# A perceiver layer on one core: tail loads merged and put before the last context slab, and two reorderings on TensorE

## The chip, the cores and the metric

The kernel runs on one core of a Trainium2 chip. A core has five engines that run side by side, each with its own list of instructions: TensorE (PE in the profile, with its weight loads as PEld), VectorE (DVE), ScalarE (ACT), GpSimd (POOL) and SyncE (SP). SP does no arithmetic here: it issues the loads, one after another, and a load that has to wait holds up all behind it. Sixteen DMA engines carry them out. The metric is the time of the whole program on the device in microseconds (us), lower is better.

## The reference: what is computed

Eight batches of 64 rows of 512 numbers (`x`) go through one layer, all in float32:

```
x = x + cross_attention(layernorm(x), context)      # one head of 512; context: 8 x 1601 rows of 512
x = x + resonance_attention(layernorm(x))           # 16 heads of 32, sigmoid in place of softmax
x = x + experts(layernorm(x))                       # 8 experts, each row goes to its best one
```

In the cross attention of a batch the scores are `(q Wq + bq)(ctx Wk + bk)^T / sqrt(512)`; a softmax runs over the 1601 context rows, and the result is the weighted sum of `ctx Wv + bv`. Only this part reads the context, 3.3 MB a batch, and it is where most of the change lies.

## The kernel before

The 512 rows of x are four tiles of 128 rows, so a tile holds a pair of batches (`p` = 0 to 3, `b2` = 0 or 1 in it). The projections with Wk and Wv are moved out of the context: the queries are multiplied by Wk (`keyed`), the scores are taken against the raw context, and the weighted sum of raw context rows is multiplied by Wv afterwards (`at_out`, matmuls named `p_po`).

**Context.** 1601 rows of a batch are 12 x 128 and 65 more. The first 1536 come in three slabs of 1 MB (`cx_p_g_b2`, groups g = 0, 1, 2), each 128 partitions by four rows. The 65 rest (group 3, the tail) are spread over four blocks of 32 partitions as 17, 16, 16 and 16 rows (`REST`) in a tile that POOL filled with zeros at the start (L205). Tails have two sets of tiles; pair p uses set p % 2.

**Loads.** `load_group` issues them on the SP queue. For pair 0 the order is weights and x, then the slabs of groups 0, 1, 2 (both batches each), then eight tail loads. For later pairs `load_pair` issues groups 0, 1, tails, 2. A slab's buffer comes from a pool of twelve, so a later load also waits until its buffer's last reader is done. Three tiny POOL copies named `held` (L931) stand between the first readings of two buffers and their reuse by pair 1.

**Transposes.** The scores need the context with its 512 columns on the partitions. DVE transposes 32 x 32 blocks (`turn_group`, L245 for slabs, L252 for tails) into tiles `T_p_q_b2`, q = 0 to 3 a quarter of the columns. A quarter's tile is complete when groups 0, 1, 2 and 3 are in it. For pair 0 the order of DVE's work at the beginning is written out by hand: groups 0 and 1 for all quarters, then groups 2 and 3 for quarters 0 and 1, and then for quarters 2 and 3 (`turn_first`).

**Scores.** `scores` (L411) multiplies quarter by quarter into four PSUM banks `sc`, the two batches in the two halves of the rows. For quarter 0 of pair 0 it does the first 256 columns of each bank early (groups 0 and 1) and the rest (`lo=256`: group 2 and the tail) later; between them PE computes `qb` (L379, `biased`).

**Softmax and sum.** `softmax` takes the maximum on DVE and the exponential on ACT into L. `chances` transposes a group of L on PE (L457, `pp`) and copies it to `pt` on ACT (L459). `attend` (L467, `ac`) multiplies it with the raw slabs. In the gap while ACT computes the exponentials, PE does other work: for p = 1 and 2 the projection of the pair before (`at_out`, L187), into whose middle the first `chances` is put.

**The other parts.** The steps of the second attention and of the experts (`unit_q`, `values`, `split`, `flip` and so on) run on tiles two pairs behind, between these. After pair 3 a list of `do(...)` lines gives PE's order: `split` transposes q and k (`t_q`, `t_k`), `flip` transposes rows that were gathered for the experts (`t_xe`), ACT copies them to `xeT` (L1087), and `up_first` multiplies them (`gu`, L1097). The rows come by DMA from a buffer in HBM, into which POOL scattered them, behind the loads of the expert weights (`fetch`, L1083).

PE's order is the program's text order throughout. DVE's and ACT's are so in marked stretches and are planned by the framework elsewhere.

Of the kernel before, what the change touches and what calls it, by code (L numbers as in the profile page):

```python
# [10 lines left out]
F32 = mybir.dt.float32  # L11
# [6 lines left out]
P = 128  # L18
B, S, D = 8, 64, 512
# [17 lines left out]
def perceiver_kernel(ctx: ExitStack, tc: tile.TileContext, out: bass.AP, t: dict):  # L37
    nc = tc.nc
# [8 lines left out]
    one = pool(name="one", bufs=1)  # L47
# [3 lines left out]
    def slab(name):  # L51
        return slabs.tile([P, DC, D], F32, tag="slab", name=name)
# [4 lines left out]
    def row4(name):  # L57
        return rowp.tile([P, DC, P], F32, tag="row", name=name)
# [54 lines left out]
    bq, _ = load_c("xbq", [P, DC], nc.scalar)  # L113
# [68 lines left out]
    def projected(srcT, w, name, between=None):  # L182
# [14 lines left out]

    scale = 1.0 / math.sqrt(D)
    tails = [
        [one.tile([P, D], F32, tag=f"tail{k}{b2}", name=f"tail{k}{b2}") for b2 in range(2)]  # L200
        for k in range(2)
    ]
    for k in range(2):
        for b2 in range(2):
            nc.gpsimd.memset(tails[k][b2], 0.0)  # L205


    REST = (17, 16, 16, 16)
    def load_group(p, g):
        got = []  # L210
        for b2 in range(2):
            src = t["ctx"][2 * p + b2]
            if g < 3:
                c = slab(f"cx_{p}_{g}_{b2}")
                rows = src[: 12 * P, :].rearrange("(q c) d -> q c d", c=12)
                ins = nc.sync.dma_start(out=c, in_=rows[:, 4 * g : 4 * g + 4, :])
                if p == 1 and g == 0:
                    tc.keep_in_program_order(ins)
            else:
                c = tails[p % 2][b2]  # L220
                k0 = 12 * P
                for a, n in enumerate(REST):
                    ins = nc.sync.dma_start(
                        out=c[32 * a : 32 * a + n, :], in_=src[k0 : k0 + n, :]
                    )
                    if p < 2:
                        tc.keep_in_program_order(ins)
                    k0 += n
            got.append(c)
        return got  # L230

    cxs = {}
    for g in (0, 1, 2, 3):
        cxs[0, g] = load_group(0, g)


    NB = D // 32
    WIDTH = tuple(384 + n for n in REST)

# [3 lines left out]
    def turn_group(T, p, q, b2, g):  # L243
        if g < 3:
            nc.vector.transpose(  # L245
                T[:, :, 128 * g : 128 * g + 128].rearrange("p b (c k) -> p b c k", k=32),
                cxs[p, g][b2][:, :, 128 * q : 128 * q + 128].rearrange(
                    "p c (b d) -> p b c d", d=32
                ),
            )  # L250
        else:
            ins = nc.vector.transpose(  # L252
                T[:, :, 384:416],
                cxs[p, 3][b2][:, 128 * q : 128 * q + 128].rearrange("p (b d) -> p b d", d=32),
            )
            if p > 1:
                tc.keep_in_program_order(ins)
# [71 lines left out]
        T = slabs.tile([P, DC, D], F32, tag="slab", name=f"T_0_{q}_{b2}")  # L329
        first[q, b2] = T[:, :, :416]  # L330

    def turn_first(g, qs=range(4)):
        for b2 in range(2):
# [10 lines left out]
    for g in (0, 1):  # L344
        turn_first(g)
# [48 lines left out]
    def queries(p):  # L394

        return one.tile([P, NB, P], F32, tag="R", name=f"R_{p}")
# [8 lines left out]
    def scores(p, q, R, sc, Ts, js=range(4), lo=0, hi=D):  # L405
        for j in js:
            b = 4 * q + j
            for a in range(4):
                for b2 in range(2):
                    r = b2 * S  # L410
                    nc.tensor.matmul(  # L411
                        sc[a][r : r + S, lo : min(hi, WIDTH[a])],
                        lhsT=R[32 * a : 32 * a + 32, b, r : r + S],
                        rhs=Ts[b2][32 * a : 32 * a + 32, j, lo : min(hi, WIDTH[a])],
                        start=(b == 0 and lo == 0), stop=(b == NB - 1),
                    )

    def softmax(p, sc):
# [13 lines left out]
        for a in range(4):  # L432
# [4 lines left out]
            )  # L437
        for a, n in enumerate(REST):
            nc.scalar.activation(
# [13 lines left out]
    def chances(p, g, L):  # L453
        nch = 4 if g < 3 else 1
        tp = bank4(f"pp_{p}_{g}")
        for j in range(nch):
            nc.tensor.transpose(tp[:, j, :], L[:, 4 * g + j, :], ident)  # L457
        pt = row4(f"pt_{p}_{g}")
        nc.scalar.copy(pt[:, :nch, :], tp[:, :nch, :])  # L459
        return pt  # L460
# [433 lines left out]
    def at_out(i, between=None):  # L894
        project(i, tile_of[i]["acT"], between)
# [7 lines left out]
    def load_pair(p):  # L903

        for g in (0, 1, 3, 2):
            cxs[p, g] = load_group(p, g)
# [4 lines left out]
    def do(*steps):  # L911
        for f, i in steps:
            f(i)
# [29 lines left out]
            for q in qs:  # L943
                turn_group(second[q, b2], 1, q, b2, g)

    for qs in (range(2), range(2, 4)):
        for g in (2, 3):
            turn_first(g, qs)
    scores(0, 0, R, sc, [first[0, 0], first[0, 1]], lo=256)
    first[3, 1] = blocks(0, 3, 1)  # L950
    for q in range(1, 4):
# [7 lines left out]
    for p in range(NT):  # L959
# [32 lines left out]
        r = over_sum()  # L992
# [4 lines left out]
        def chance():  # L997
            pts.append(chances(p, len(pts), L))
# [6 lines left out]
        if p == 0:  # L1005
            chance()
            tables()
            keep_keyed(1, qk)
            R = queries(1)
        elif p + 1 < NT:  # L1010
            R = queries(p + 1)
            if p == 1:
                qk = keyed(NT - 1)
            at_out(p - 1, chance)
            if p == 1:
                keep_keyed(NT - 1, qk)
        else:
            at_out(p - 1, chance)
        if 0 < p < NT - 1:
# [126 lines left out]
    fetch(0)  # L1146
    load_experts_late(gu, dn)
    do((unit_q, 2), (at_turn, 3), (unit_k, 2), (at_out, 3), (norm, 3), (gates, 2))
    do((values, 2), (flip, 0), (split, 2), (up_first, 0), (turn, 3), (align, 2), (up_last, 0))
    do((unit_q, 3), (over, 0), (sums, 2))  # L1150
    unit_k(3, lambda: back(2))
    do((flip, 1), (output, 2))
# [134 lines left out]
```

## Time and profile before

| | us |
|---|---|
| median of three runs (lowest, highest) | 288.14 (286.54, 288.61) |
| the profiled execution | 286.62 |
| its span, first to last instruction | 284.7 |
| PE busy in the span | 270.7 |
| DVE, ACT, POOL busy | 159.1, 113.4, 70.5 |
| clock that PE was granted | 0.998 of full speed |

The span is shorter than the time by 1.9 us, which lie around the first and the last instruction. Busy time says that an engine had an instruction running, not that it ran at its peak. An idle gap is given with what ended it ("<-DVE T L252" is: until DVE's instruction of line 252 wrote tile T). Names stand as output<-inputs; "x64" counts instructions; each float32 matmul of the program appears as two. A row of several instructions has been merged, and its time is from the first start to the last end.

### The profile page before, as it was taken

How to read it: one execution, taken by the hardware profiler on the slowest of the kernel's cores; microseconds unless marked ns; L12 is line 12 of the kernel's file. 1: busy time of each engine (PE TensorE's matmuls, PEld its weight loads, DVE VectorE, ACT ScalarE, POOL GpSimd, SP SyncE). 2: the span in 40 equal slices, each digit the busy share in tenths (PEclk: the TensorE clock that was granted, in tenths of full speed). 3: DMA queues.
4: the chain of work that ended last, by engine and by line, in shares of the span. 5: the costliest groups of instructions: out<-in, count | busy, mean ns of one | idle time of the engine just before them, and what ended most of it. 6: DMA issues, size and time to landing. Idle time of an engine off the chain costs nothing. (4 is left out here: it accounts for less than half of the span.)

```text
span 284.7 us, 6695 instructions
## 1 busy us (share of the span) xinstructions
PE 270.7 (95%) x2724; PEld 136.0 (48%) x2724; DVE 159.1 (56%) x422; ACT 113.4 (40%) x244; POOL 70.5 (25%) x120
## 2 busy tenths in 40 slices
PE   6999699999999999999999999999999999999990
PEld 5975548335643345644434564434444555442320
DVE  3576729359432987846688765631562476384130
ACT  2574006980176522267744047534326424130210
POOL 3351560000971004060220400031140041404211
PEclk9999999999999999999999999999999999999999
DMA  6997686399799980000897036299980200614501
GB/s 210 423 416 308 196 290 236 92 423 395 265 316 397 383 321 9 6 0 0 315 361 284 2 146 211 92 294 367 359 309 2 76 0 2 211 48 149 151 0 45
DMA packets 20177, 57.72 MB, mean 203 GB/s; under 512 B 2418, under 2 KB 10658, under 8 KB 16432
## 3 DMA queue, kind: packets, MB, share of 16 engines
q1 hardware_dynamic: 17568, 50.37, 48.2%
q0 software_dynamic: 2432, 6.89, 6.9%
q8 instruction: 23, 0.38, 0.6%
q14 instruction: 10, 0.08, 0.1%
q10 hardware_dynamic: 144, 0.00, 0.0%
HBM read 50.94 MB, written 6.84 MB: 203 GB/s over the span
## 5 line engine op out<-in xcount | busy, mean ns | idle before, releaser
L245 DVE STREAM_TRANSPOSE T<-cx 128x512 f32<-128x512 f32 x96 | 61.5, 678 | 19.0 <-DMA cx<-in_ctx_dram 18.6
L411 PE MATMUL sc<-T,R 32*64 32x400 f32 (+4 forms) x1088 | 48.1, 480 | 2.4 <-DVE T L252 2.3
L467 PE MATMUL ac<-cx,pt 128*64 128x512 f32 x192 | 43.8, 598 | 0.1
L411 PEld LDWEIGHTS sc<-T,R 32*64 32x64 f32 x1088 | 24.1, 131 | 21.0 <-issue 14.6
L401 ACT COPY R<-qkT 32x512 f32<-32x512 f32 x40 | 24.6, 616 | 0.7
L467 PEld LDWEIGHTS ac<-cx,pt 128*64 128x64 f32 x192 | 12.7, 136 | 22.2 <-issue 21.4
L1097 PE MATMUL gu<-wgu,xeT 128*32 128x512 f32 x192 | 22.8, 597 | 0.0
L544 POOL TENSOR_TENSOR gm_k<-qn_k,c_gk 128x512 f32<-128x512 f32 x4 | 5.1, 1282 | 60.0 <-DVE qn_k L539 60.0
L401 POOL COPY R<-qkT 32x512 f32<-32x512 f32 x24 | 14.5, 605 | 17.4 <-PE sc L411 10.9
L422 DVE TENSOR_REDUCE mx<-sc 128x1 f32<-128x400 f32 (+1 forms) x16 | 8.1, 568 | 13.5 <-PE sc L411 13.5
L187 PE MATMUL p_po<-w_xWv,acT 128*128 128x512 f32 x32 | 14.9, 592 | 0.0
L359 PE MATMUL qk<-qpT,w_xWkT 128*128 128x128 f32 (+1 forms) x96 | 14.8, 311 | 0.0
L187 PE MATMUL p_q<-w_aWq,xhT 128*128 128x512 f32 x32 | 14.8, 606 | 0.0
L187 PE MATMUL p_k<-w_aWk,xhT 128*128 128x512 f32 x32 | 14.7, 595 | 0.0
L315 PE MATMUL qp<-xnT,w_xWq 128*128 128x128 f32 (+1 forms) x64 | 14.5, 383 | 0.1
L187 PE MATMUL p_o<-w_aWo,cT 128*128 128x512 f32 x32 | 14.5, 596 | 0.0
L187 PE MATMUL p_v<-w_aWv,xvT 128*128 128x512 f32 x32 | 14.4, 592 | 0.0
L507 POOL TENSOR_TENSOR x<-x,c_bo 128x512 f32<-128x512 f32 x4 | 5.1, 1273 | 36.3 <-DVE xh L506 36.3
L359 PEld LDWEIGHTS qk<-qpT,w_xWkT 128*128 128x128 f32 x96 | 13.4, 191 | 1.4 <-issue 0.6
L459 ACT COPY pt<-pp 128x512 f32<-128x512 f32 (+1 forms) x16 | 8.2, 510 | 10.4 <-PE pp L457 10.3
L315 PEld LDWEIGHTS qp<-xnT,w_xWq 128*128 128x128 f32 x64 | 9.7, 191 | 4.5 <-ACT xnT L304 0.4
L1132 PE MATMUL y<-wd,hT 128*32 128x512 f32 x96 | 11.5, 596 | 0.3 <-ACT hT L1124 0.3
(197 smaller groups left out, 371.3 us busy)
## 6 DMA issues: line engine op xcount, KB each, us to landing
cx<-in_ctx_dram SPq DMA_DIRECT2D x24, 1024.0 KB, 8.5
wgu<-in_wgT_dram SPq DMA_DIRECT2D x8, 512.0 KB, 9.9
wgu<-in_wuT_dram SPq DMA_DIRECT2D x8, 512.0 KB, 7.1
wd<-in_wdT_dram SPq DMA_DIRECT2D x8, 512.0 KB
rd<-blank POOLq DMA_DIRECT2D x6, 258.0 KB, 6.1
in<-rd SPq DMA_DIRECT2D x6, 258.0 KB, 4.2
xd<-blank POOLq DMA_DIRECT2D x6, 256.0 KB, 5.8
in<-xd SPq DMA_DIRECT2D x6, 256.0 KB, 7.1
```

The lines of the kernel that those rows point to most:

```text
L187: nc.tensor.matmul(ps, lhsT=srcT[:, dc, :], rhs=w[:, dc, :], start=(dc == 0), stop=(dc == DC - 1),)
L245: nc.vector.transpose(T[:, :, 128 * g : 128 * g + 128].rearrange("p b (c k) -> p b c k", k=32), cxs[p, g][b2][:, :, 128 * q : 128 * q + 12 ...
L315: nc.tensor.matmul(ps[ec][:, : n * P], lhsT=wq[:, dc, ec * P : (ec + 1) * P], rhs=xnT[:, dc, cols], start=(dc == 0), stop=(dc == DC - 1),)
L359: nc.tensor.matmul(ps[c * n // DC][:, c % (DC // n), :, :], lhsT=wkT[:, ec, c * P : (c + 1) * P], rhs=qpT[:, ec, cols], start=(ec == 0), s ...
L401: copy(R[32 * a : 32 * a + 32, j::4, :], qkT[32 * j : 32 * j + 32, :, :])
L411: nc.tensor.matmul(sc[a][r : r + S, lo : min(hi, WIDTH[a])], lhsT=R[32 * a : 32 * a + 32, b, r : r + S], rhs=Ts[b2][32 * a : 32 * a + 32, ...
L422: nc.vector.tensor_reduce(mx[:, a : a + 1], sc[a][:, : WIDTH[a]], AX.X, ALU.max)
L459: nc.scalar.copy(pt[:, :nch, :], tp[:, :nch, :])
L467: nc.tensor.matmul(ac[r : r + S, :], lhsT=pt[:, j, r : r + S], rhs=cx[b2][:, j, :] if g < 3 else cx[b2], start=(g == 0 and j == 0), stop=( ...
L507: nc.gpsimd.tensor_tensor(xs[i], xs[i], bo, ALU.add)
L1097: nc.tensor.matmul(ps[c, :], lhsT=xTs[k][:, dc, c], rhs=ffw[e][0][:, dc, :], start=(dc == 0), stop=(dc == DC - 1),)
L1132: nc.tensor.matmul(y[c, :], lhsT=hT[:, ic, c], rhs=ffw[e][1][:, ic, :], start=(ic == 0), stop=(ic == IC - 1),)
```

## The change

Three edits. The first merges the two batches' tail tiles of a set into one tile `[128, 2, 512]`, filled by four loads (17, 16, 16, 16 rows by two batches) in place of eight. For pair 0 those four are issued ahead of the slab of group 2 of the second batch, and DVE's order there becomes: group 2 of batch 0 for quarters 0 to 2, tails of both batches for quarters 0 and 1, group 2 of batch 1 for quarters 0 to 2, tails for quarter 2, then quarter 3. Later pairs keep their order of groups. The second edit: for p = 2 the first `chances` follows the whole projection instead of standing in its middle; p = 1 and 3 stay. The third: `split` of tile 2 stands ahead of `flip` of the first gathered rows. In the built program, the instructions on PE, DVE, ACT, POOL and SP are otherwise in the same order; ACT's copy of `t_q` comes ahead of that of `t_xe`.

```diff
     tails = [
-        [one.tile([P, D], F32, tag=f"tail{k}{b2}", name=f"tail{k}{b2}") for b2 in range(2)]
-        for k in range(2)
+        one.tile([P, 2, D], F32, tag=f"tail{k}", name=f"tail{k}") for k in range(2)
     ]
     for k in range(2):
-        for b2 in range(2):
-            nc.gpsimd.memset(tails[k][b2], 0.0)
+        nc.gpsimd.memset(tails[k], 0.0)
...
+    def load_tails(p):
+
+        c = tails[p % 2]
+        k0 = 12 * P
+        for a, n in enumerate(REST):
+            ins = nc.sync.dma_start(
+                out=c[32 * a : 32 * a + n, :, :],
+                in_=t["ctx"][2 * p : 2 * p + 2, k0 : k0 + n, :].rearrange("b r d -> r b d"),
+            )
+            if p < 2:
+                tc.keep_in_program_order(ins)
+            k0 += n
+        return [c[:, b2, :] for b2 in range(2)]
+
     def load_group(p, g):
...
+        return [load_chunks(p, g, b2) for b2 in range(2)] if g < 3 else load_tails(p)
 
     cxs = {}
-    for g in (0, 1, 2, 3):
+    for g in (0, 1):
         cxs[0, g] = load_group(0, g)
+    cxs[0, 2] = [load_chunks(0, 2, 0)]
+    cxs[0, 3] = load_group(0, 3)
+    cxs[0, 2].append(load_chunks(0, 2, 1))
...
-    def turn_first(g, qs=range(4)):
-        for b2 in range(2):
+    def turn_first(g, qs=range(4), batches=range(2)):
+        for b2 in batches:
...
-    for qs in (range(2), range(2, 4)):
-        for g in (2, 3):
-            turn_first(g, qs)
+    turn_first(2, range(3), (0,))
+    turn_first(3, range(2))
+    turn_first(2, range(3), (1,))
+    turn_first(3, (2,))
+    for g in (2, 3):
+        turn_first(g, (3,))
     scores(0, 0, R, sc, [first[0, 0], first[0, 1]], lo=256)
...
-            at_out(p - 1, chance)
             if p == 1:
+                at_out(p - 1, chance)
                 keep_keyed(NT - 1, qk)
+            else:
+                at_out(p - 1)
+                chance()
...
-    do((values, 2), (flip, 0), (split, 2), (up_first, 0), (turn, 3), (align, 2), (up_last, 0))
+    do((values, 2), (split, 2), (flip, 0), (up_first, 0), (turn, 3), (align, 2), (up_last, 0))
```

`load_chunks(p, g, b2)`, which is not shown, issues one slab as `load_group` did.

More of the change, by code (lines that the diff above doesn't have):

```diff
@@ L199, in perceiver_kernel, with load_chunks @@
     tails = [
-        [one.tile([P, D], F32, tag=f"tail{k}{b2}", name=f"tail{k}{b2}") for b2 in range(2)]
-        for k in range(2)
+        one.tile([P, 2, D], F32, tag=f"tail{k}", name=f"tail{k}") for k in range(2)
     ]
     for k in range(2):
-        for b2 in range(2):
-            nc.gpsimd.memset(tails[k][b2], 0.0)
+        nc.gpsimd.memset(tails[k], 0.0)
     REST = (17, 16, 16, 16)
-    def load_group(p, g):
-        got = []
-        for b2 in range(2):
[L212 to L230, printed above, removed]
+    def load_chunks(p, g, b2):
+        c = slab(f"cx_{p}_{g}_{b2}")
+        rows = t["ctx"][2 * p + b2][: 12 * P, :].rearrange("(q c) d -> q c d", c=12)
+        ins = nc.sync.dma_start(out=c, in_=rows[:, 4 * g : 4 * g + 4, :])
+        if p == 1 and g == 0:
+            tc.keep_in_program_order(ins)
+        return c
+    def load_tails(p):
[7 more added lines that the diff above has]
+            if p < 2:
+                tc.keep_in_program_order(ins)
+            k0 += n
+        return [c[:, b2, :] for b2 in range(2)]
+    def load_group(p, g):
+        return [load_chunks(p, g, b2) for b2 in range(2)] if g < 3 else load_tails(p)
     cxs = {}
-    for g in (0, 1, 2, 3):
+    for g in (0, 1):
         cxs[0, g] = load_group(0, g)
+    cxs[0, 2] = [load_chunks(0, 2, 0)]
+    cxs[0, 3] = load_group(0, 3)
+    cxs[0, 2].append(load_chunks(0, 2, 1))
     NB = D // 32
@@ L330, in perceiver_kernel @@
         first[q, b2] = T[:, :, :416]
-    def turn_first(g, qs=range(4)):
-        for b2 in range(2):
+    def turn_first(g, qs=range(4), batches=range(2)):
+        for b2 in batches:
             for q in qs:
```

## The prediction

> **What bounds the kernel now.** I read the page first, then the waits of TensorE (PE), then the timeline around each wait, then the stretches of two microseconds with the DMA rate.
>
> ```profile
> PE 270.7 (95%) x2724; PEld 136.0 (48%) x2724; DVE 159.1 (56%) x422; ACT 113.4 (40%) x244; POOL 70.5 (25%) x120
> ```
>
> PE is busy for 270.7 of 284.7 us, so the kernel can only be shortened by what PE waits for: 14.0 us, of which 1.86 lie before the first matmul and about 6.5 behind the last. The list of its waits (total us, times, longest) names the rest:
>
> ```profile
> PE sc L411 <- DVE T L252: 2.3, 2, 1.5
> PE pp L457 <- ACT L L433: 0.8, 1, 0.8
> PE t_xe L179 <- DMA in<-xd: 0.6, 1, 0.6
> ```
>
> Each edit lies at one of these three. Together they hold 3.65 us, 1.3% of the time; that is the ceiling, unless an edit also moves a wait.
>
> **Edit 1: the tails.** The timeline around the first wait (start, duration, what, idle before it):
>
> ```profile
> 25.56 1.30 DVE L245 STREAM_TRANSPOSE T<-cx 128x512 f32<-128x512 f32 x2 [0.59 <-DMA cx<-in_ctx_dram]
> ...
> 28.47 0.81 PEld L379 LDWEIGHTS qb<-qpT,c_xbk 128*32 128x32 f32 x32 [0.39 <-issue]
> ...
> 28.74 1.31 DVE L245 STREAM_TRANSPOSE T<-cx 128x512 f32<-128x512 f32 x2 [1.88 <-DMA cx<-in_ctx_dram]
> ...
> 30.30 0.46 PE L411 MATMUL sc<-T,R 32*64 32x145 f32 x2 [0.74 <-DVE T L252]
> ...
> 31.90 0.51 DVE L252 STREAM_TRANSPOSE T<-tail 128x128 f32<-128x128 f32 x2 [1.47 <-DMA tail<-in_ctx_dram]
> ...
> 32.27 3.27 PEld L411 LDWEIGHTS sc<-T,R 32*64 32x64 f32 x126 [1.78 <-DVE T L252]
> ```
>
> PE has done all it can at 29.56 (L379's matmuls end there). It waits until 32.27 for the second batch's tail, which VectorE (DVE) sees at 31.90. The stretches say what the DMAs did meanwhile (last two columns: share of the 16 DMA engines, GB/s):
>
> ```profile
> 24.00:26.00 2.00, 2.00 (x8) 1.21 (x7) 1.41 (x3) 0.58 (x1) 0.00 (x0) 1.00 0.99 413
> 26.00:28.00 2.00, 2.00 (x58) 1.27 (x65) 0.87 (x2) 0.58 (x1) 0.00 (x0) 1.00 0.41 112
> 28.00:30.00 2.00, 1.55 (x56) 0.90 (x40) 1.26 (x3) 0.27 (x1) 0.00 (x0) 1.00 0.16 50
> ```
>
> All 16 engines run at 413 GB/s (25.8 each) until 26; then one or two are left. The SP queue's waits say why: its tail loads wait for context slabs to land, 25.3 us in 11 waits. An instruction list of the built program shows that every load waits for the eighth load before it, so the last tail load leaves only when the last slab has landed (28.74) and lands 3.1 us later.
>
> The change halves the tail loads (8 to 4 a pair, same 2 KB rows) and puts them ahead of the last slab. By the same counting the four now leave behind landings at 10.6 to 14.6, and the slab `cx_0_2_1` behind that of `cx_0_0_1` (16.9), all long before the queue runs dry. So the issue wait goes. What is late next is the slab, on the one engine that carries the odd rows. In the semaphore records a 17-row load has one late mark and a 16-row load has sixteen: the 17 rows sit on one engine. The packet records agree: from 27.0 to 29.7 rows of 2 KB follow one another every 83 ns.
>
> A slab lands every 2.5 us (16 engines of 64 KB at 25.8 GB/s). From the first at 14.6, the fifth (`cx_0_2_0`) is through at 24.6 on an engine without other work. Then that engine has 34 rows of the 17-row load and 6 of the other three: 80 KB, 3.2 us. Then its 64 KB of `cx_0_2_1`, 2.5 us. It lands at 30.3. The tails themselves land by about 28, and DVE turns them before the slab, in its new order. One transpose (0.67) ends at 31.0, and PE starts there instead of 32.27: **-1.25**. Behind it each quarter finds its tiles: this part takes PE about 1.1 us and a full quarter 2.8, DVE turns one tile in 0.67, and the tile built last ends at some 36, needed at 37.7.
>
> Bounds: nothing is won if the slab lands at 31.6 or later; all is won, 2.6 us (32.27 less 29.6), if the odd rows cost that engine nothing. I take 1.25, since it comes from rates measured in this very stretch.
>
> [...]
>
> Beside other work: the two big zero fills (L205) replace four; the first stands ahead of the identity on GpSimd (POOL), 1.05 us instead of 0.53, and the 15 idle turns (3.46 us, from 1.86) then end at 5.85. The transposes behind them start at 5.88, waiting for DVE. Cost 0, at most 0.5 if that cover is gone. Everything up to the second wait is paced by PE: pair 1's last slabs leave at 53.94 when PE has used a buffer, and its first ones at 30.48 when the `held` copies are through, 14 us before use. In the saturated stretch before the third pair, DVE has its first tiles by 104.6 and PE asks at 106.91: a slack of 2.3 us.
>
> **Edit 2: chances behind the projection (p = 2).**
>
> ```profile
> 125.99 1.88 PE L187 MATMUL p_po<-w_xWv,acT 128*128 128x512 f32 x4
> ...
> 128.63 0.65 PE L457 MATMUL pp<-ident,L 128*128 128x128 f32 x4 [0.75 <-ACT L L433]
> 129.12 1.88 PE L187 MATMUL p_po<-w_xWv,acT 128*128 128x512 f32 x4
> ...
> 129.37 0.59 ACT L459 COPY pt<-pp 128x512 f32<-128x512 f32 x1
> ...
> 131.80 3.65 PE L467 MATMUL ac<-cx,pt 128*64 128x512 f32 x16
> ```
>
> Four rows of `p_po` take 1.72 us from start to start. With all eight first, `pp` starts at 125.99 + 3.44 = 129.43; the last exponential ended at 128.49, so nothing waits. Then `pp` 0.49, `t_x` 0.43, the second `pp` 0.53 (starts as now), and `ac` starts at 130.88 instead of 131.80: **-0.92**. Its other condition is the copy of `pt`, which ends 1.33 us after `pp` starts: 130.76, just in time. If ScalarE (ACT) is late by more than 0.12, the excess is lost; bounds 0 and -0.92, taken -0.92. The add to x behind `p_po` comes 1.3 us earlier.
>
> **Edit 3: t_q and t_k ahead of t_xe.**
>
> ```profile
> 209.70 0.63 PE L179 MATMUL t_xe<-ident,in 128*128 128x128 f32 x4 [0.64 <-DMA in<-xd]
> ...
> 210.42 0.59 ACT L1087 COPY xeT<-t_xe 128x512 f32<-128x512 f32 x1 [2.61 <-PE t_xe L179]
> ...
> 211.13 2.06 PE L1097 MATMUL gu<-wgu,xeT 128*32 128x512 f32 x16
> ```
>
> `gu` starts 1.43 us after `t_xe`, because ACT copies in between; today `t_q` and `t_k` (0.44 each) fill just that gap. After the change they fill the wait for the rows, and the gap is bare. PE is free at 208.9 (205.46 + 8 x 0.43). New: `t_q` 208.9, `t_k` 209.34, `t_xe` 209.8, `gu` 211.23: **+0.10**. Had the rows landed by 208.9, it would cost 0.9; if they land after 209.8, 0. The rows move with PE, since the stream of expert weights that they queue behind starts at 184.03 when PE releases a buffer.
>
> **Sum.** -1.25 - 0.92 + 0.10 = -2.07 us. The profiled execution took 286.62 us (span 284.7 and 1.9 around it): 284.6. It lies 1.5 below the median of the three other runs (288.14); against the mean of all four, 287.5, the forecast is **285.4 us**.
>
> **Rivals.**
> 1. The odd rows don't hold the slab up. For: only 50 GB/s move after 28, so room is there; against: the one late mark. -2.6 - 0.92 + 0.1 = -3.4: 284.1.
> 2. The change doesn't do what it says at the tails: that engine is hit by something else (ring 8 moved 16 KB in 1.2 us at 29.45) and the slab lands at 31.6. Only edits 2 and 3 are left, -0.8: 286.7.
> 3. The gain sinks at `t_xe`: if the weights' stream is bound by DMA and not by PE, the rows land no earlier, and `gu` starts where it did: 287.5. For: the stream runs at 294 to 367 GB/s in three slices of the page; against: its start at 184.03.
> 4. Slower: the 40 rows ahead of the slab take longer than 83 ns. In the crowd at 26.5 to 26.9 single ones took 150. At that rate the slab lands at 24.6 + 6.0 + 2.5 = 33.1, PE starts at 33.8, +1.5 - 0.8 = +0.7: 288.2. It decides from 133 ns a row, where the loss reaches the 0.8 of the others.
>
> **Chances and range.** Forecast 0.48; rival 1 0.20; 2 0.12; 3 0.10; 4 0.10. A measurement of this kernel tells about 1% (2.9 us) from no change; its four runs span 2.1 us. Faster by over 1%: rival 1 in most cases and the upper edge of the forecast, 0.24. Slower by over 1% needs rival 4 at more than twice its price: 0.07. Within: 0.69. The range 283.2 to 288.0 goes from rival 1 with the lower runs of the kernel to rival 3; it leaves out most of rival 4 and the far ends of the scatter.
>
> **What would show it.** Right: one PE wait of about 1.4 us in front of `sc`, released by the transpose of `cx`, not of `tail`; DMA share near full until 27; no wait at `pp`; `ac` 4.9 us behind the start of `p_po`; no wait at `t_xe` but one of some 0.8 at `gu` on ACT. Wrong: `sc` running on from L379 without a wait, a wait there past 32.3, or a longer wait at `t_xe`.

## The result

| | before | after |
|---|---|---|
| median of 20 runs each, us | 286.71 | 288.15 |
| lowest, highest | 284.76, 288.61 | 286.14, 290.21 |
| the profiled execution | 286.62 | 289.25 |
| its span | 284.7 | 287.1 |

The ratio is 1.0059 with a 95% interval of 1.0033 to 1.0085: the change makes the kernel about 0.6% slower. (The ratios, here and below, are those on record; they aren't the quotients of the medians beside them.) Forecast were 285.4 us and a range that ends at 288.0.

The page of the kernel after, its line of busy times and one of its lines of 40 slices:

```profile
PE 273.6 (95%) x2724; PEld 138.6 (48%) x2724; DVE 159.3 (55%) x422; ACT 113.3 (39%) x244; POOL 70.4 (25%) x118
...
PEclk9999779999999999999999999999999999999998
```

PE is busy for 273.6 us where it was for 270.7, with the same 2724 matmuls. The row PEclk says why: in two slices of 7.2 us, from 28.7 us on, it had 0.7 of its clock.

The list of PE's waits in the kernel after:

```profile
PE sc L415 <- DVE T L249: 2.4, 2, 2.2
...
PE sc L415 <- DVE T L256: 0.7, 1, 0.7
PE gu L1107 <- ACT xeT L1097: 0.7, 1, 0.7
```

The waits at `pp` and `t_xe` are gone. At `sc` there are 3.1 us of waiting where there were 2.3, and the long one is now for the transpose of a slab (L249), not of a tail (L256). The timeline around it (start, duration, what, idle before it):

```profile
27.10 1.90 DVE L249 STREAM_TRANSPOSE T<-cx 128x512 f32<-128x512 f32 x3 [2.02 <-DMA cx<-in_ctx_dram]
...
30.02 0.89 DVE L256 STREAM_TRANSPOSE T<-tail 128x128 f32<-128x128 f32 x4 [1.02 <-DMA tail<-in_ctx_dram]
...
30.39 0.46 PE L415 MATMUL sc<-T,R 32*64 32x145 f32 x2 [0.68 <-DVE T L256]
...
32.28 1.90 DVE L249 STREAM_TRANSPOSE T<-cx 128x512 f32<-128x512 f32 x3 [1.36 <-DMA cx<-in_ctx_dram]
...
33.05 6.82 PE L415 MATMUL sc<-T,R 32*64 32x145 f32 x126 [2.20 <-DVE T L249]
...
39.80 0.33 PE L395 MATMUL t_qb<-ident,qbT 128*128 128x128 f32 x1
```

Two things went wrong. The slab `cx_0_2_1` lands at 32.25 (semaphore record), so PE starts the second part of `sc` at 33.05 instead of 32.27: 0.78 later than before. And the 126 matmuls that follow take 6.82 us; before, the same 126 took 3.96:

```profile
32.27 3.96 PE L411 MATMUL sc<-T,R 32*64 32x145 f32 x126 [1.52 <-DVE T L252]
```

The stretches of two microseconds of the kernel after (PE, PEld, DVE, ACT, POOL busy, then PE's granted clock, share of the DMA engines, GB/s):

```profile
31.00:33.00 2.00, 0.00 (x0) 0.00 (x0) 0.72 (x2) 0.00 (x0) 2.00 (x5) 0.79 0.71 156
33.00:35.00 2.00, 1.96 (x63) 1.96 (x71) 2.00 (x5) 0.00 (x0) 1.54 (x3) 0.50 1.01 408
35.00:37.00 2.00, 2.00 (x36) 1.44 (x31) 1.99 (x6) 0.00 (x0) 0.00 (x0) 0.50 0.96 270
37.00:39.00 2.00, 2.00 (x32) 1.42 (x24) 0.45 (x1) 0.00 (x0) 0.31 (x1) 0.50 1.00 381
39.00:41.00 2.00, 2.00 (x48) 0.88 (x40) 0.16 (x1) 0.00 (x0) 2.00 (x2) 1.00 0.45 144
```

From 32.2 to 39.0 us PE had half its clock (the clock's own record). In the profile of before, the wait ends at 32.27 and every stretch there shows 1.00.

So the profiled execution sums up as +0.78 (slab), +2.86 (clock), -0.98 (edit 2) and -0.09 (edit 3): +2.57, against a last matmul that ends 2.61 later. The two GB/s columns show the slab's lateness beginning much earlier. Before, from 24 to 27 us:

```profile
24.00:25.00 1.00, 1.00 (x5) 0.60 (x4) 0.97 (x2) 0.58 (x1) 0.00 (x0) 1.00 1.00 418
25.00:26.00 1.00, 1.00 (x5) 0.60 (x4) 0.44 (x1) 0.00 (x0) 0.00 (x0) 1.00 0.99 408
26.00:27.00 1.00, 1.00 (x18) 0.42 (x25) 0.87 (x2) 0.33 (x1) 0.00 (x0) 1.00 0.70 185
```

and after:

```profile
24.00:25.00 1.00, 1.00 (x4) 0.57 (x3) 1.00 (x2) 0.58 (x1) 0.00 (x0) 1.00 1.16 211
25.00:26.00 1.00, 1.00 (x5) 0.59 (x4) 0.08 (x1) 0.00 (x0) 0.00 (x0) 1.00 0.88 248
26.00:27.00 1.00, 1.00 (x14) 0.42 (x20) 0.00 (x0) 0.17 (x1) 0.00 (x0) 1.00 1.03 330
```

The engines are as busy as before and move half as much. This is not one engine with a queue of odd rows, which was my picture: all of them are slow. Packets of 8 KB of the slabs, which take 309 to 321 ns at 21 to 23 us, took 540 to 850 ns when they began at 24 to 25 us, and the slab ahead of the tails, `cx_0_2_0`, lands at 27.08 instead of 25.54. A slab has sixteen marks in the semaphore records, and its landing is the last. Fifteen marks of `cx_0_2_0` come by 24.35 before and by 25.17 after; the last one lags behind the others in both kernels, by 1.2 us from 20.6 us on. That this comes from a packet of 16 KB of the instruction queue, which the DMA records show at 16.4 us before and 16.8 after, is read from the order of times. The experiments ask three things: what each edit does alone, why the stream slows down, and what the clock is worth.

### The profile page after: what moved, and what is told of

Its sections match the earlier page's. It is cut to its first block, busy times and chain, and to the rows that moved or that the text cites. A ratio compares the mean times of both kernels' runs of the same rounds, so it can differ in the third digit from the quotient of the medians.

```text
span 287.1 us, 6661 instructions
## 1 busy us (share of the span) xinstructions
PE 273.6 (95%) x2724; PEld 138.6 (48%) x2724; DVE 159.3 (55%) x422; ACT 113.3 (39%) x244; POOL 70.4 (25%) x118
## 5 line engine op out<-in xcount | busy, mean ns | idle before, releaser
L249 DVE STREAM_TRANSPOSE T<-cx 128x512 f32<-128x512 f32 x96 | 61.5, 679 | 20.2 <-DMA cx<-in_ctx_dram 19.8
L415 PE MATMUL sc<-T,R 32*64 32x400 f32 (+4 forms) x1088 | 51.0, 506 | 3.1 <-DVE T L249 2.4
L415 PEld LDWEIGHTS sc<-T,R 32*64 32x64 f32 x1088 | 25.9, 141 | 22.7 <-issue 15.9
L405 ACT COPY R<-qkT 32x512 f32<-32x512 f32 x40 | 24.6, 616 | 0.7
```

What stands on the lines that cost most here:

```text
L249: nc.vector.transpose(T[:, :, 128 * g : 128 * g + 128].rearrange("p b (c k) -> p b c k", k=32), cxs[p, g][b2][:, :, 128 * q : 128 * q + 12 ...
L405: copy(R[32 * a : 32 * a + 32, j::4, :], qkT[32 * j : 32 * j + 32, :, :])
L415: nc.tensor.matmul(sc[a][r : r + S, lo : min(hi, WIDTH[a])], lhsT=R[32 * a : 32 * a + 32, b, r : r + S], rhs=Ts[b2][32 * a : 32 * a + 32, ...
```

## Experiments: each edit alone

The first three runs each make one edit of the diff and leave the rest as before.

> Edit 1 alone; edits 2 and 3 are taken back. Theory A (the loss is all in the tails: the slab behind the odd rows lands later than the last tail did, 0.8 us, and the longer wait of TensorE is followed by a window of some 6.8 us at half clock, 2.9 us): 2.5 to 3.7 us slower than before in the executions that show the half clock, about 0.8 slower in those that don't; one such window visible between 33 and 40 us. Theory B (the loss comes from edits 2 or 3): within 1 us of before.

Measured: median 288.06 against 287.05 (35 runs of before), ratio 1.0057 (1.0025 to 1.0090). Edit 1 alone costs as much as all three edits together. Theory A holds in direction and place; its 2.5 to 3.7 us for the executions with half clock came out as some 1.1 against before's with it and 2.6 against before's without. Its waits at `sc` are 2.2 and 0.8 us, its slabs land at 27.16 and 32.18, and its profile has half a clock for 3.4 us from 33.8.

> Edit 2 alone. Theory A: 0.9 us faster than before, no wait of TensorE at the first pp of p = 2, clock as before. Theory B: as slow as or slower than before.

Measured: 284.87, ratio 0.9949 (0.9917 to 0.9981). The wait at `pp` is gone, and this edit alone is a gain of half a per cent, 0.5 to 2.4 us by the interval. Predicted were 0.9.

> Edit 3 alone. Theory A: within 0.3 us of before; the wait at t_xe (0.64) is gone and one of some 0.7 stands at gu behind the copy xeT. Theory B: slower by up to 2 us.

Measured: 286.77, ratio 0.9995 (0.9964 to 1.0026): no difference that can be told. The wait at `t_xe` is gone, and one of 0.7 us at `gu` stands in its place. The three ratios together make no change, where the whole change has 1.0059; with intervals of 0.3% each, that difference isn't clear of the noise.

## Experiments: the odd rows

The next run makes all three edits, but issues the odd row by itself, so that no load has 17 rows:

```diff
-        for a, n in enumerate(REST):
+        at = [(32 * a, k0 + 16 * a + (a > 0), 16) for a in range(4)] + [(16, k0 + 16, 1)]
+        for r0, k0, n in at:
```

> The changed kernel with all three edits, but the 17-row load of each tail split into 16 rows and 1 row, so that no DMA engine carries 34 rows; five loads a pair in place of four, same bytes. Theory A (the odd rows on one engine hold the last slab up, and the long wait brings the half clock): cx_0_2_1 lands by 29.5 instead of 32.3, TensorE waits under 1 us in front of the second part of quarter 0, no half-clock window, 2.5 to 3.5 us faster than before and 4 to 5 faster than the changed kernel's profiled execution. Rival C (the slab is late for another reason: the instruction fetch on one engine, or its later issue): it lands at 31 to 32 as in the changed kernel, and the half clock stays.

Measured: 284.61, ratio 0.9946 (0.9912 to 0.9979). `cx_0_2_1` lands at 30.51 instead of 32.25 and PE starts at 31.30, so the 17-row load on one engine costs 1.74 us. But the slab lands later than theory A's 29.5, the wait at `sc` is 1.4 us and not under 1, and the gain is 1.5 us by the ratio where 2.5 to 3.5 were expected. The rate is no better either (220 GB/s from 23 to 26 us) and `cx_0_2_0` still lands at 27.28. So there are two troubles: the odd rows, and something in all the tail loads.

Another run keeps edit 2 alone of the others, and puts the merged tails, odd row apart, behind both slabs, with DVE's order to match:

```diff
-    cxs[0, 2] = [load_chunks(0, 2, 0)]
+    cxs[0, 2] = load_group(0, 2)
     cxs[0, 3] = load_group(0, 3)
-    cxs[0, 2].append(load_chunks(0, 2, 1))
```

> A version from what the runs showed: edit 2, the merged tail tile with its odd row as a load of its own (five loads a pair), but for pair 0 behind both slabs of group 2 as in the kernel before, and VectorE turning the tiles of quarter 0 first; edit 3 left out. Theory A with E or F (tails in the stream cost the slabs 1.6 us, the odd rows 1.8, the waits for earlier loads the rest): cx_0_2_0 lands at 25.5 and cx_0_2_1 at 28.7 as before, the tails by 29.5, TensorE starts the second part of quarter 0 by 30.3, 2 us earlier than before; with edit 2 the sum is 2.5 to 3.5 us faster than before, 283.6 to 284.6. If the tails land no earlier than 31 us, only edit 2 is left: 285.9 to 286.2.

Measured: 285.18, ratio 0.9949 (0.9921 to 0.9978). `cx_0_2_0` lands at 25.28, `cx_0_2_1` at 29.46, the last tail at 30.25 (before: 31.78), the last two later than theory A had them, and PE waits once at `sc`:

```profile
30.91 4.90 PE L414 MATMUL sc<-T,R 32*64 32x145 f32 x128 [1.05 <-DVE T L255]
```

PE starts 1.36 us earlier than before, but takes 4.90 us for what it then did in 4.42 (0.46 and 3.96), with gaps in between, and `t_qb` is only 0.42 earlier. Neither this version nor the one with the odd row apart is measurably better than edit 2 alone; where the latter's gain goes is told at the end.

## Experiments: why the stream slows down

All runs of this section are the changed kernel with other loads of the tails; only the traffic is compared. Each was run and profiled once (284.0 to 286.7 us). How far one profile can be trusted is seen where the same loads were profiled more than once: before, edit 2 alone, edit 3 alone and the filled kernel before (e6_before_filled, below) have 408 to 418 GB/s from 23 to 26 us and land the slabs at 25.49 to 25.64 and 28.72 to 28.92; the change, edit 1 alone and the filled change (e5_filled) have 238 to 270 GB/s, 26.96 to 27.16 and 32.05 to 32.25. The first has one load of 64 rows of each batch, to every other partition:

```diff
-        for a, n in enumerate(REST):
-            ins = nc.sync.dma_start(
-                out=c[32 * a : 32 * a + n, :, :],
-                in_=t["ctx"][2 * p : 2 * p + 2, k0 : k0 + n, :].rearrange("b r d -> r b d"),
-            )
+        ins = nc.sync.dma_start(
+            out=c[0:P:2, :, :],
+            in_=t["ctx"][2 * p : 2 * p + 2, k0 : k0 + 64, :].rearrange("b r d -> r b d"),
+        )
```

> The changed kernel with the four tail loads of a pair replaced by one load of 64 of the 65 rows of both batches to every other of the 128 partitions; same row size, the odd row left out, and the rows stand at other places than the computation needs (the tail's part of the scores and sums is another one). Theory E (the tails slow the whole stream because each load writes to 16 neighbouring partitions only): 400 GB/s and more hold through 23 to 27 us, cx_0_2_0 lands by 25.6 and cx_0_2_1 by 29. Theory F (rows of 2 KB with their own order slow it, wherever they go): the rate falls to 150 to 250 GB/s around 24 us as in the changed kernel, and cx_0_2_0 lands at 27.

One load to every other partition leaves the stream as it was: 412 GB/s from 23 to 26 us, the slabs at 25.81 and 28.92, and no wait for a tile at `sc` above 0.2 us. My first reading was that rows to neighbouring partitions are slow (theory E). The next two have four loads of 16 rows, to every eighth partition, and as the change has them:

```diff
-        for a, n in enumerate(REST):
+        for a in range(4):
...
-                out=c[32 * a : 32 * a + n, :, :],
+                out=c[a:P:8, :, :],
```

> The changed kernel, its tail loads replaced by four loads of 32 rows each (16 rows of each batch) that go to partitions a, a + 8, a + 16, ..., so to every eighth partition; the odd row of each batch is left out and the rows stand at other places than the computation needs, so only the traffic is meant. Theory E (rows that go to neighbouring partitions slow the whole stream): 400 GB/s or more from 23 to 26 us as before the change, cx_0_2_0 lands by 25.8 and cx_0_2_1 by 29.0 us, no wait at sc above 1 us. Theory F (any four loads of 2 KB rows between the slabs do it, wherever the rows go): 150 to 350 GB/s from 24 to 26 us, cx_0_2_0 lands at 27 and cx_0_2_1 at 30 or later, a wait at sc of about 2 us.

```diff
-                out=c[32 * a : 32 * a + n, :, :],
+                out=c[32 * a : 32 * a + 16, :, :],
```

> The control: the same four loads of 32 rows, to 16 neighbouring partitions each, as the change has them; the odd row of each batch is left out. Theory E and theory F alike: 150 to 350 GB/s from 24 to 26 us, cx_0_2_0 lands at about 27.1 and cx_0_2_1 at about 30.3 us. If instead it lands by 29.0 with 400 GB/s kept, it is the odd rows in the 17-row load alone that slow the stream, and both theories fall.

Theory E fell: every eighth partition slows the stream too (262 GB/s, 27.09 and 30.50), though less than neighbours do (204 GB/s, 27.77 and 31.00, later than either theory had it).

F met its bounds for the stream and the slabs there; the wait at `sc` was 1.1 us, not 2. Then four loads to every fourth partition, and one load to 64 neighbours:

```diff
-                out=c[a:P:8, :, :],
+                out=c[a:64:4, :, :],
```

> As the run with every eighth partition, but the 16 rows of each of the four loads go to every fourth partition (a, a + 4, ..., a + 60); the odd row of each batch is left out and the rows stand at other places than the computation needs. With every eighth partition the rate fell to 223 GB/s at 24 to 25 us and the slab landed at 30.50, so neighbouring partitions alone are not the cause. Theory G (a load of 16 rows is slow where its rows fall on few of the memory's paths, and both 16 neighbours and every eighth do that while every fourth doesn't): 400 GB/s or more from 23 to 26 us, cx_0_2_0 lands by 25.8 and cx_0_2_1 by 29.0 us, no wait at sc above 1 us. Theory F (small loads of 16 rows of 2 KB slow the stream wherever their rows go): 150 to 350 GB/s from 24 to 26 us, cx_0_2_0 lands at about 27 and cx_0_2_1 at about 30.5 us.

```diff
-            out=c[0:P:2, :, :],
+            out=c[0:64, :, :],
```

> One load of 64 rows of each batch in place of four, to the 64 neighbouring partitions 0 to 63; the odd row of each batch is left out and the rows stand at other places than the computation needs. Theory E (neighbouring partitions): 150 to 350 GB/s from 24 to 26 us, cx_0_2_0 at about 27, cx_0_2_1 at 30 us or later. Theory F (small loads) and theory G (few paths) alike: 400 GB/s or more until 26 us, cx_0_2_0 lands by 25.8 and cx_0_2_1 by 29.0 us, as the one load to every other partition did (25.81 and 28.92).

Every fourth partition is slow as F has it, but less (332 GB/s, 26.38 and 29.98); G's bounds are missed, and its paths are a supposition that no run shows. The single load to 64 neighbours is slow too (272 GB/s, 26.59 and 30.21), against F and G both. So it can't be only that the loads are small, and not the neighbours alone either. Four loads to every seventh partition came next:

```diff
-                out=c[a:P:8, :, :],
+                out=c[a : a + 106 : 7, :, :],
```

> As the runs with every eighth and every fourth partition: four loads of 16 rows of each batch, here to every seventh partition (a, a + 7, ..., a + 105); the odd row of each batch is left out and the rows stand at other places than the computation needs. [...] Theory F (four small loads cost more than one, wherever the rows go): as with every eighth or fourth partition, cx_0_2_0 at 26.4 to 27.1 and cx_0_2_1 at 30.0 to 30.5 us.

Measured: 325 GB/s, 26.73 and 29.83, far from the one load to every other partition (412, 25.81 and 28.92); F missed its last bound by 0.2 us. The places of the one harmless load were then filled by four loads and by two:

```diff
-                out=c[a:P:8, :, :],
+                out=c[2 * a : P : 8, :, :],
```

> The same places as the one load to every other of the 128 partitions (which left the stream at 412 GB/s from 23 to 26 us and landed the slabs at 25.81 and 28.92), but filled by four loads of 16 rows of each batch, each to every eighth partition (0, 2, 4 and 6 onwards). The odd row of each batch is left out and the rows stand at other places than the computation needs. Theory H (what counts is that all the rows together fall evenly on all parts of the memory): 380 GB/s or more from 23 to 26 us, cx_0_2_0 by 26.1 and cx_0_2_1 by 29.4 us. Theory F (small loads between the slabs disturb the stream wherever they go): at most 340 GB/s, cx_0_2_0 at 26.4 to 27.2 and cx_0_2_1 at 29.7 to 30.6 us.

```diff
-        for a in range(4):
+        for a in range(2):
...
-                out=c[2 * a : P : 8, :, :],
-                in_=t["ctx"][2 * p : 2 * p + 2, k0 : k0 + 16, :].rearrange("b r d -> r b d"),
+                out=c[2 * a : P : 4, :, :],
+                in_=t["ctx"][2 * p : 2 * p + 2, k0 : k0 + 32, :].rearrange("b r d -> r b d"),
```

> The same places again, filled by two loads of 32 rows of each batch, each to every fourth of the 128 partitions (0 and 2 onwards). The odd row of each batch is left out and the rows stand at other places than the computation needs. Theory H: as the one load, 380 GB/s or more, 25.8 to 26.1 and 28.9 to 29.4 us. Theory F: between the one load and four, 340 to 390 GB/s, cx_0_2_0 at 26.0 to 26.6 and cx_0_2_1 at 29.3 to 29.9 us.

By four loads: 318 GB/s, 26.39 and 29.67. By two: 410 GB/s, 25.71 and 28.85. So evenness of the sum (H) isn't enough, and the step from two loads to four, which F expected to be gradual, is a jump. What was left: it counts where the rows of each load by itself go, or loads of 16 rows are bad anywhere (F). Four loads again, moved by 32 partitions against e11_step4:

```diff
-                out=c[a:64:4, :, :],
+                out=c[32 + a : 96 : 4, :, :],
```

> The four loads to every fourth partition again (there 0 to 63: 332 GB/s from 23 to 26 us, slabs at 26.38 and 29.98), shifted by 32 partitions (32 + a, 36 + a, ..., 92 + a) and nothing else. [...] The odd row of each batch is left out and the rows stand at other places than the computation needs. [...] Theory F (loads of 16 rows disturb the stream wherever they go): at most 345 GB/s, cx_0_2_0 at 26.3 or later and cx_0_2_1 at 29.6 us or later.

And two loads of 32 rows, as in e17_two, but to every other of the partitions 0 to 63:

```diff
-                out=c[2 * a : P : 4, :, :],
+                out=c[a:64:2, :, :],
```

> [...] The odd row of each batch is left out and the rows stand at other places than the computation needs. [...] Theory F: as the two loads before, 380 GB/s or more, cx_0_2_0 by 26.0 and cx_0_2_1 by 29.2 us.

These two decide it. The stretch from 23 to 26 us with four loads to the partitions 0 to 63, every fourth:

```profile
23.00:26.00 3.00, 3.00 (x11) 1.81 (x10) 2.18 (x4) 0.73 (x2) 0.00 (x0) 1.00 1.04 332
```

and with the same four loads moved by 32 partitions, to 32 to 95:

```profile
23.00:26.00 3.00, 3.00 (x11) 1.81 (x10) 2.38 (x5) 0.75 (x2) 0.00 (x0) 1.00 1.02 412
```

The last column goes from 332 to the full 412 GB/s, and the slabs land at 25.75 and 28.87. Nothing but a start of 32 was added. Two loads of 32 rows to half the partitions, every other from 0 to 63, which F took for harmless:

```profile
23.00:26.00 3.00, 3.00 (x11) 1.80 (x10) 2.23 (x4) 0.77 (x2) 0.00 (x0) 1.00 1.08 254
```

They land the slabs at 27.07 and 30.62. F missed all its bounds in both runs, so what counts here is where the rows of each load go. By the rate:

| partitions of a load | loads | GB/s, 23 to 26 us | `cx_0_2_0` | `cx_0_2_1` |
|---|---|---|---|---|
| before: no tails there | 0 | 414 | 25.54 | 28.72 |
| every other of 128 (e7_spread) | 1 | 412 | 25.81 | 28.92 |
| every fourth, 32 to 95 (e18_shift) | 4 | 412 | 25.75 | 28.87 |
| every fourth of 128 (e17_two) | 2 | 410 | 25.71 | 28.85 |
| every fourth, 0 to 63 (e11_step4) | 4 | 332 | 26.38 | 29.98 |
| every seventh (e13_step7) | 4 | 325 | 26.73 | 29.83 |
| every eighth, 0, 2, 4, 6 (e16_four) | 4 | 318 | 26.39 | 29.67 |
| 64 neighbours (e12_one64) | 1 | 272 | 26.59 | 30.21 |
| the change: 16 neighbours, odd rows on one engine | 4 | 270 | 27.08 | 32.25 |
| every eighth, 0 to 3 (e9_step8) | 4 | 262 | 27.09 | 30.50 |
| every other, 0 to 63 (e19_two8) | 2 | 254 | 27.07 | 30.62 |
| 16 neighbours (e10_step1) | 4 | 204 | 27.77 | 31.00 |

The runs show which places are harmless, and not why. Above all the shift by 32 shows it: the same four loads have 332 GB/s from partition 0 on and 412 from 32 on. That it would help was a supposition ahead of the run; no run shows by which way the rows of a load reach their partitions. The loss doesn't hang on the one engine that lags: the middle one of the sixteen marks of `cx_0_2_1` comes at 27.2 to 27.3 in the three runs with 410 GB/s and more and tails in the stream, at 27.9 to 28.7 in the six with 254 to 332, and at 29.6 in e10_step1 with 204 (in the change, where one engine carries the whole 17-row load, at 28.6). Within the six the order isn't explained. The runs show besides that the slabs, which go to all partitions, are held up with the tails, the one that was issued before them too (`cx_0_2_0` at 26.38 to 27.77 in the eight slow rows of the table, 25.54 before), and that every seventh partition, from 0 to 108 over the four loads, does no better than every fourth from 0 to 63 (325 GB/s against 332).

## Experiments: the clock

Two runs keep PE turning during the wait, with identity transposes whose results nobody reads: 28 in the changed kernel, ahead of L415's second part, and 20 in the kernel before.

```diff
+    idle_turns(28)
     scores(0, 0, R, sc, [first[0, 0], first[0, 1]], lo=256)
```

> The changed kernel with 28 transposes of the identity into an unused bank (0.112 us each, 3.1 us) between qb and the second part of quarter 0, where TensorE waits for 29.7 to 33.0 us. Nothing that arrives is any earlier. Theory A (the low activity in that wait brings half-clock windows of 3.4 us): no such window in the profile, the 126 rows of sc there take 4.0 us instead of 6.8, and the median falls by 1.2 to 2.5 us, to 285.7 to 287.0. Theory D (the clock falls for a reason that has nothing to do with the wait): windows and median as in the changed kernel, 288.

Measured: 288.06, ratio 1.0046 (1.0023 to 1.0069). By their mean clock none of its 12 runs has a stretch of half clock in mid-run, and the 128 rows of `sc` take 3.98 us. Yet the median is as high as the change's.

> The kernel before with 20 such transposes (2.2 us) at the same place, where TensorE waits from 29.6 to 32.3 us. Theory A: the executions of before that lose a half-clock window go, the median falls by 0.5 to 1.2 us, to 285.9 to 286.6, and the scatter shrinks. Theory D: no difference.

Measured: 286.93, ratio 1.0020 (0.9993 to 1.0047). Its runs lie closer together (285.74 to 287.91 against 284.43 to 288.64) and are not faster in the middle: the expected gain didn't come.

In both runs the transposes themselves stood in PE's way. In e5_filled the first tile of the slab was turned by 32.75, but PE started `sc` at 33.87, behind the last transpose; in e6_before_filled quarter 0 was turned by 31.2, and `sc` started at 33.29. So about 1 and 2 us went into the filling. Besides, `t_qb` starts 2.03 us earlier in e5_filled's profile than in the change's and the last matmul ends only 0.76 earlier: 0.72 is lost between `t_qb` and `qk`, and 0.69 in a wait at `sc` at 74.1 us. The two runs show what the idle time does to the clock, and not what the stretch is worth.

What the clock costs can still be read from the runs by their mean granted clock, since profiles with such a stretch show 0.984 to 0.992 and those without it 0.993 to 0.998:

| | runs with half clock in mid-run | median with | without |
|---|---|---|---|
| before (two sets) | 27 of 64 | 287.45, 287.75 | 286.00, 285.98 |
| after | 17 of 20 | 288.25 | 286.72 |
| edit 1 alone | 8 of 12 | 288.59 | 287.10 |
| odd row apart (e4_even) | 2 of 12 | 286.85 | 284.54 |
| edit 2 alone | 2 of 12 | 286.67 | 284.74 |
| edit 3 alone | 3 of 12 | 288.34 | 286.73 |
| tails behind (e8_behind) | 2 of 12 | 286.17 | 284.99 |
| after, filled (e5_filled) | 0 of 12 | - | 288.06 |
| before, filled (e6_before_filled) | 1 of 12 | 287.06 | 286.85 |

A stretch goes with 1.2 to 2.3 us more in every kernel that isn't filled, and the change has it twice as often as before: 0.85 less 0.42, times 1.5, is some 0.65 of the 1.44 us between the medians. This price is a comparison of executions, not of kernels. The rest of the 1.44 is not accounted for: the slab's 0.78 and the 0.25 around the span (see the end) are made up for by the 1.07 that edits 2 and 3 won in the profile, so some 0.8 us stay open.

That PE's idle time at `sc` brings the stretch about is shown by filling it: 0 of 12 runs against 17 of 20, and 1 of 12 against 27 of 64. Its length tells too: with a longest wait of 2.0 to 2.2 us in the profile (after, edit 1 alone) 25 of 32 runs have a stretch; with before's loads and waits (before, edits 2 and 3 alone; longest 1.2 to 1.6) 32 of 88; with one of 1.0 to 1.4 and no other above 0.3 (odd row apart, tails behind) 4 of 24.

## Why the prediction was wrong

**Edit 1, the landing of the slab: wrong.** The failed term is "34 rows of the 17-row load and 6 of the other three: 80 KB, 3.2 us", at 83 ns a row. The odd rows do sit on one engine, as predicted. Followed back from the end, its 40 rows stand one behind the other from 23.7 to 29.3: 5.6 us and 140 ns a row. Then come its 64 KB of the slab in 2.5 us, and the slab lands at 32.25, 0.4 behind their last packet; PE started at 33.05 where -1.25 meant 31.0. Rival 4 had the mechanism and a chance of 0.10: at 140 ns its sum gives 24.6 + 5.6 + 2.5 = 32.7, half a microsecond late, since the engine was free for the rows earlier than the sum has it. That rival 4's total, 288.2, is the measured one is luck: it starts from 287.5, the mean of four runs, where twenty have a median of 286.71, and it holds no loss by the clock. I had the 83 ns from a time when almost no slab was in flight, and took them for a crowded one; the 150 ns that stood in the same trace were the better row. The crowd isn't all of it: from 28.3 to 28.8 us, with 45 GB/s moving, rows took 160 to 166 ns, and why stays open. Part of the loss has another cause than the rival's: with the odd row apart the slab still landed at 30.51, 1.6 us behind the 28.87 of e18_shift, whose stream isn't slowed, by where the 16-row loads go.

**What the prediction didn't have: the clock.** Its sums hold PE's durations fixed. The term "this part takes PE about 1.1 us and a full quarter 2.8" became 6.82 us for what had taken 3.96, which is the largest single item of the profiled difference. That the clock would stay whole was put in without a reason. The page of before shows 0.998 in the one execution that was profiled, but of 64 later executions of the same kernel 27 had the stretch.

**Edit 2: right.** Predicted -0.92; measured -0.98 in the profile, and ratio 0.9949 alone, whose interval holds the 0.92. That its median lies 2.2 us below before's is in part luck: 2 of its 12 runs have the half clock, which sets in some 90 us ahead of this edit's place. PE in the kernel after:

```profile
129.62 3.60 PE L187 MATMUL p_po<-w_xWv,acT 128*128 128x512 f32 x8
133.05 0.60 PE L461 MATMUL pp<-ident,L 128*128 128x128 f32 x4
133.49 0.60 PE L179 MATMUL t_x<-ident,x 128*128 128x128 f32 x4
133.92 0.60 PE L461 MATMUL pp<-ident,L 128*128 128x128 f32 x4
134.45 2.79 PE L471 MATMUL ac<-cx,pt 128*64 128x512 f32 x12
```

`ac` starts 4.83 us behind the start of `p_po`, where 4.9 was forecast, and nothing waits.

**Edit 3: right in mechanism.** Predicted +0.10, measured -0.09. The gap moved as described:

```profile
212.42 0.60 PE L179 MATMUL t_xe<-ident,in 128*128 128x128 f32 x4
213.05 0.58 ACT L1097 COPY xeT<-t_xe 128x512 f32<-128x512 f32 x1 [0.23 <-PE t_xe L179]
...
213.69 2.11 PE L1107 MATMUL gu<-wgu,xeT 128*32 128x512 f32 x16 [0.67 <-ACT xeT L1097]
```

`gu` starts 1.27 us behind `t_xe`, where 1.43 had been copied from before.

**The smaller points.** The zero fills cost nothing: the idle turns start 0.42 later and `t_xn` 0.17 earlier. Rival 3 didn't happen: `t_xe` has no wait for its rows. The marks "one PE wait of about 1.4 us", "DMA share near full until 27" came out as a wait of 2.2 and a full share at half the rate; "a wait there past 32.3" is what was named as the sign of being wrong.

## What to carry to other kernels

Before a small load is put into a saturated stream, look at which partitions its rows go to: here four loads to every fourth partition from 32 to 95 left the slabs at 25.75 and 28.87 (25.54 and 28.72 without tails there), and the same bytes to 16 neighbours landed them 2 us later, at 27.77 and 31.00. Take the duration of a packet from a stretch as crowded as the one it will be in: a row had 83 ns in the kernel before, where some 50 GB/s moved, and 140 ns on the mean in the crowd of the kernel after. And judge a change to a PE wait of 2 to 3 us from many runs: whether half a clock follows it differs from execution to execution (17 of 20 with the change, 27 of 64 before), and that is worth more than the 0.78 us by which the wait's end moved here. A filling that is to keep PE busy has to end before the data is there, or it takes back part of what it saves (about 1 us in e5_filled and 2 us in e6_before_filled).

## What was not expected of the hardware

**The clock's stretches** came in units of 3.4 us: 3.4 in the profiles of edit 1 alone, edit 3 alone and e10_step1, 6.8 in the kernel after, always at 0.50 of full speed, and each near the wait at `sc`. In edit 3 alone that wait is as in the kernel before (2.4 us in two parts), so a wait of this length sometimes brings it and sometimes not. The traces show what goes with it: counted off in units of 3.41 us from where PE first has its full clock (by the clock's record 7.07 us in the profile of before, 8.27 in that of after), each stretch begins at the end of a unit in which PE was busy for little, 1.03 us in edit 3 alone, 1.23 in edit 1 alone, 1.42 in the kernel after and 1.78 in e10_step1; in the profiles without a stretch no unit before 270 us has less than 2.07, and before's lowest is 2.10. In the kernel after the stretch begins 23.89 us behind that point, 7.0 units, and the half clock at the very end of before, behind the last matmul, 276.48 us, 81.0 units. So by this count, whether a wait brings a stretch hangs on where the units fall on it; that this is what differs between executions of one kernel is not shown, since only one of each was profiled. The kernel after kept half a clock for a second unit; there PE was still idle for 0.89 us of the first, and in the other three it was busy throughout. (Units of 1.47 us at the end of before and of 1.67 us at the end of e16_four aren't followed by half a clock, so no sharp limit can be given.) PE didn't stand still for a whole unit in the kernel after: the longest gap was 2.2 us, with 0.46 us of matmuls and another gap of 0.7 ahead of it.

**Instructions that come late.** Where PE got past the wait earlier, part of the gain was lost behind it. With the four loads to every fourth partition from 32 on (e18_shift) PE doesn't wait at `sc` at all, and its timeline is:

```profile
29.55 4.07 PE L415 MATMUL sc<-T,R 32*64 32x145 f32 x128
33.55 0.33 PE L395 MATMUL t_qb<-ident,qbT 128*128 128x128 f32 x1
33.81 5.60 PE L415 MATMUL sc<-T,R 32*64 32x401 f32 x120
39.99 0.90 PE L415 MATMUL sc<-T,R 32*64 32x400 f32 x8 [0.58 <-issue]
40.82 2.42 PE L363 MATMUL qk<-qpT,w_xWkT 128*128 128x256 f32 x10
```

`t_qb` starts 2.61 us earlier than before, `qk` only 1.16: a gap put down to "issue", so to nothing that the profile shows waiting, stands in front of the same instruction in four runs. The DMA records have a packet of 16 KB of the instruction queue just before it:

| | `t_qb` | packet ends | PE goes on | `t_qb` to `qk` |
|---|---|---|---|---|
| before | 36.16 | 39.63 | no gap | 5.82 |
| e19_two8 | 35.30 | 39.08 | no gap | 5.84 |
| e16_four | 34.35 | 38.68 | no gap shown | 6.48 |
| e12_one64 | 34.90 | 39.61 | 40.94 | 6.88 |
| e17_two | 33.99 | 39.19 | 40.56 | 7.39 |
| e7_spread | 33.60 | 38.59 | 39.99 | 7.22 |
| e18_shift | 33.55 | 38.76 | 39.99 | 7.27 |

PE goes on 1.2 to 1.4 us behind the packet's end each time. In e16_four, e13_step7 and e11_step4 (`t_qb` at 34.35 to 34.66) the rows of PE show no gap above 0.3 us, but `t_qb` to `qk` is 0.5 to 0.7 longer than before and the same instruction stands 1.3 to 1.5 us behind the packet; in no profile does it come sooner than 1.2 us behind it. So up to 1.6 us of what is won at `sc` is lost again some five microseconds later. That the packet is what PE waits for is read from the order of times; no run moved it alone. It would help to explain why e18_shift (284.50 in its one run) is no faster than the version with the odd row apart (284.61), whose `t_qb` is at 35.19 and whose `t_qb` to `qk` is 6.29.

**Left open:** why the time around the span is 0.25 us longer in the kernels with edit 1 as it stands (2.14 us and 2.21, against 1.9): in every run with four tail loads a pair it is 2.08 us or more, while with five, two or one it is 1.76 to 1.93 in all but two runs of e8_behind. And why a load's places matter as they do: why the shift by 32 takes four loads from 332 to 412 GB/s, and why every seventh partition stays at 325.
